# Layer 0's projection as a seven-product Strassen form, with the first phase's other steps moved between engines

## The chip, the cores and the metric

The kernel runs on one core of one Trainium2 chip. A core has five engines with an instruction queue each: TensorE (PE; its weight loads are PEld) multiplies matrices into PSUM, VectorE (DVE) and ScalarE (ACT) work elementwise from SBUF and PSUM, GpSimd (POOL) works elementwise in SBUF, and SyncE (SP) issues most of the DMAs. Each queue runs in its own order; engines wait for one another on semaphores.

The metric is the device time of one execution in microseconds. Before the change it is 2088.59 us, the median of 3 runs (2086.69 to 2091.08).

## What is computed

128 graphs of 128 nodes with 256 features, all float32, pass two layers. Each layer is followed by a residual sum and a layer norm. The change concerns layer 0:

```python
norm = (adj.sum(-1) + 1e-6) ** -0.5                 # per node
f_hom = norm * (adj @ (norm * (x @ theta)))
f_het = x @ W_h
gate  = sigmoid(x @ W_t + b_t)
x1    = layernorm(x + elu(gate * f_hom + (1 - gate) * f_het))
```

Layer 1 takes x1 through a pointwise convolution with batch norm, a convolution of 17 taps along the nodes, a message product weighted by exp(-distance) and a GRU. In this kernel the 17-tap convolution is done in the frequency domain along the nodes.

## The kernel before

**Three phases.** The first (profile time 0 to about 746 us) does layer 0, the pointwise convolution `conv1`, the forward transform (coefficients `H`) and the transform of the convolution weights. The second (to about 960 us) multiplies coefficients and transformed weights, frequency by frequency; its operands come over DMA. The third (to the end) does the inverse transform, messages and the GRU; its GRU projections already use a seven-product Strassen form (`l1_sums`, `l1_gru`, L762 to L805), with 384-column products and with sums on VectorE and GpSimd.

**The first phase's loop** (L436 to L483) runs over turns `t`. A pair `p` is two graphs, so there are 64 pairs, and a turn works on several of them at once, in software pipelining: projection, gate and mix of pair `t`, the rest of layer 0 of pair `t-1`, layer norm, transposition and `conv1` of pair `t-2`, coefficients of pair `t-3`, loads of pair `t+2`, transposition and degrees of pair `t+1`. In about every second turn `w_unit` (L403) transforms one of 32 units of convolution weights: four products on a quarter of the array's rows each (`w_ps`), one for the rest (`wl_ps`), four evictions on ScalarE, one on VectorE. `w_store` writes them out in 16 DMAs a turn later.

**Order.** For TensorE the order is that of the source in all turns (`manual_schedule`). From turn 3 on SyncE, VectorE and ScalarE have the source's order too, while GpSimd is left to the scheduler; in the turns before, a scheduler places all engines but TensorE.

**The projection** (`l0_project`, L291). For each graph, x transposed is multiplied by theta and W_h together (512 columns, `f_ps`) and by W_t (256 columns, `gate_ps`), each over two halves of the 256 features. A float32 product is two passes over the array, so a trace shows two records for each. ScalarE evicts hom, scaled by norm, and het; VectorE adds the gate's bias (L315); ScalarE takes the tanh.

**What follows it.** `l0_mix` (L324) multiplies by adj and scales by norm, less het; `l0_gate` (L339) blends, and takes the minimum and the exponential for elu; `l0_elu` (L348) adds x, then moments and the reciprocal deviation come from `norm_stats` (L242: VectorE statistics, then two small operations on GpSimd in `inv_sqrt`, L150); `norm_apply` (L253) forms the shift `nb` on VectorE and applies it on ScalarE. `l1_turn`, `l1_front` and `l1_analyse` are layer 1's share. `transposed` (L265) turns a pair on TensorE and evicts the result on VectorE (L274), for xT and for x1T.

**Memory.** All PSUM tiles of the phase rotate through 8 banks of one pool:

```python
ps = actx.enter_context(tc.tile_pool(name="psA", bufs=8, space=PSUM, reuse_waits="tile"))
```

x and adjT have four buffers each (`io`), hom, het and gate two; x1 has its own tile with one.

Of the kernel before, what the change touches and what calls it, by code (L numbers as in the profile page):

```python
# [33 lines left out]
def gnn_layers_kernel(ctx: ExitStack, tc: tile.TileContext, a: dict, out: bass.AP):  # L34
# [58 lines left out]
    ps = actx.enter_context(tc.tile_pool(name="psA", bufs=8, space=PSUM, reuse_waits="tile"))  # L93
# [8 lines left out]
    def load(p):  # L102
        s = st[p] = {}
        s["x"] = io.tile([P, J, D], F32, tag="x", name=f"x_{p}")
        nc.sync.dma_start(s["x"], x[p * J : (p + 1) * J].rearrange("b n d -> n b d"))
        s["adjT"] = io.tile([P, J, P], F32, tag="adjT", name=f"adjT_{p}")
        nc.sync.dma_start(s["adjT"], adjT[:, p * J : (p + 1) * J, :])
# [134 lines left out]
    def norm_stats(src, n, name):  # L242

        mv = small.tile([P, n, 2], F32, tag=f"mv{n}", name=f"mv_{name}")
        for q in range(n):
            stats = small.tile([P, 6], F32, tag="stats", name=f"stats_{name}_{q}")
            nc.vector.bn_stats(stats, src[:, q, :])
            nc.vector.bn_aggr(mv[:, q, :], stats)  # L248
        rstd = small.tile([P, n], F32, tag=f"rstd{n}", name=f"rstd_{name}")
        inv_sqrt(rstd, mv[:, :, 1], LN_EPS, n)  # L250
        return mv, rstd

    def norm_apply(src, dst, n, name, mv, rstd):  # L253
        nb = small.tile([P, n], F32, tag=f"nb{n}", name=f"nb_{name}")
        nc.vector.scalar_tensor_tensor(nb, mv[:, :, 0], -1.0, rstd, ALU.mult, ALU.mult)  # L255
        for q in range(n):
            nc.scalar.activation(  # L257
                dst[:, q, :], src[:, q, :], AF.Identity,
                bias=nb[:, q : q + 1], scale=rstd[:, q : q + 1],
            )  # L260
# [4 lines left out]
    def transposed(src, dst, name):  # L265
# [8 lines left out]
        nc.vector.tensor_copy(dst.rearrange("p c n -> p (c n)"), t)  # L274


    def l0_turn(p):
        s = st[p]
        s["xT"] = wk.tile([P, NC, J * P], F32, tag="xT", name=f"xT_{p}")
        transposed(s["x"], s["xT"], f"xT_{p}")  # L280
        deg = bank(f"deg_{p}")
        for j in range(J):
            nc.tensor.matmul(
                deg[:, j : j + 1], lhsT=s["adjT"][:, j, :], rhs=ones[:, 0:1], start=True, stop=True
            )
        norm = s["norm"] = small.tile([P, J], F32, tag="norm", name=f"norm_{p}")
        nc.vector.tensor_copy(norm, deg[:, 0:J])
        inv_sqrt(norm, norm, DEG_EPS, J)


    def l0_project(p, between, beside):  # L291
        s = st[p]
        xT, norm = s["xT"], s["norm"]
        hom = wk.tile([P, J, D], F32, tag="hom", bufs=2, name=f"hom_{p}")
        het = wk.tile([P, J, D], F32, tag="het", bufs=2, name=f"het_{p}")
        gate = wk.tile([P, J, D], F32, tag="gate", bufs=2, name=f"gate_{p}")
        pg = bank(f"gate_ps_{p}")
        for j in range(J):
            if j == 1:
                between()  # L300
            pf = bank(f"f_ps_{p}_{j}")
            for c in range(NC):
                nc.tensor.matmul(  # L303
                    pf, lhsT=xT[:, c, nodes(j)], rhs=w0[:, c, 0 : 2 * D],
                    start=(c == 0), stop=(c == NC - 1),
                )
            for c in range(NC):
                nc.tensor.matmul(  # L308
                    pg[:, j * D : (j + 1) * D], lhsT=xT[:, c, nodes(j)],
                    rhs=w0[:, c, 2 * D : 3 * D], start=(c == 0), stop=(c == NC - 1),  # L310
                )
            nc.scalar.activation(hom[:, j, :], pf[:, 0:D], AF.Copy, scale=norm[:, j : j + 1])  # L312
            nc.scalar.activation(het[:, j, :], pf[:, D : 2 * D], AF.Copy)
        beside()
        nc.vector.tensor_tensor(  # L315
            gate, pg.rearrange("p (j e) -> p j e", j=J),
            b_t.unsqueeze(1).to_broadcast([P, J, D]), ALU.add,
        )

        nc.scalar.activation(gate, gate, AF.Tanh, scale=0.5)  # L320
        s.update(hom=hom, het=het, gate=gate)


    def l0_mix(p):  # L324
        s = st[p]
        adjT_, norm, hom, het = (s[k] for k in ("adjT", "norm", "hom", "het"))
        pm = bank(f"mix_ps_{p}")
        for j in range(J):
            nc.tensor.matmul(  # L329
                pm[:, j * D : (j + 1) * D], lhsT=adjT_[:, j, :], rhs=hom[:, j, :],  # L330
                start=True, stop=True,
            )
        for j in range(J):
            nc.vector.scalar_tensor_tensor(
                hom[:, j, :], pm[:, j * D : (j + 1) * D], norm[:, j : j + 1], het[:, j, :],
                ALU.mult, ALU.subtract,
            )

    def l0_gate(p):  # L339
        s = st[p]  # L340
        hom, het, gate = (s[k] for k in ("hom", "het", "gate"))

        nc.vector.scalar_tensor_tensor(hom, gate, 1.0, hom, ALU.add, ALU.mult)
        nc.vector.scalar_tensor_tensor(het, hom, 0.5, het, ALU.mult, ALU.add)
        nc.vector.tensor_scalar_min(gate, het, 0.0)
        nc.scalar.activation(gate, gate, AF.Exp)

    def l0_elu(p):  # L348
        s = st[p]
        x_, hom, het, gate = (s[k] for k in ("x", "hom", "het", "gate"))  # L350

        nc.vector.scalar_tensor_tensor(gate, gate, -1.0, x_, ALU.add, ALU.add)
        nc.vector.scalar_tensor_tensor(hom, het, 0.0, gate, ALU.max, ALU.add)
        s["stats"] = norm_stats(hom, J, f"a{p}")

    def l0_norm(p):
        s = st[p]
        s["x1"] = wk.tile([P, J, D], F32, tag="x1", name=f"x1_{p}")
        norm_apply(s["hom"], s["x1"], J, f"a{p}", *s["stats"])


    def l1_turn(p):
        s = st[p]
        s["x1T"] = wk.tile([P, NC, J * P], F32, tag="x1T", name=f"x1T_{p}")
        transposed(s["x1"], s["x1T"], f"x1T_{p}")

    def l1_front(p):
        s = st[p]
        h = s["h"] = wk.tile([P, J, D], F32, tag="h", name=f"h_{p}")
        for j in range(J):  # L370
            ph = bank(f"conv1_ps_{p}_{j}")
            for c in range(NC):
                nc.tensor.matmul(  # L373
                    ph[:, 0 : D + CO], lhsT=s["x1T"][:, c, nodes(j)], rhs=conv1_w[:, c, :],
                    start=(c == 0), stop=(c == NC - 1),
                )
            nc.vector.tensor_tensor(h[:, j, :], ph[:, 0:D], shift1, ALU.add)
            nc.scalar.activation(coords[:, p * J + j, :], ph[:, D : D + CO], AF.Copy)
        nc.scalar.activation(h, h, AF.Relu)

    def l1_store(p):
        s = st[p]
        nc.sync.dma_start(x1_d[p], s["x1"].rearrange("p j e -> p (j e)"))
# [19 lines left out]
    def w_unit(u):  # L403
        t = wt[u % NW].rearrange("p i o -> p (i o)")
        pq = [bank(f"w_ps_{u}_{r}") for r in range(4)]
# [24 lines left out]


# [4 lines left out]
    for t in range(-1, NP + 3):  # L436
        with tc.manual_schedule(engines={E.PE, E.SP, E.DVE, E.Activation} if t > 2 else {E.PE}):
# [5 lines left out]
            def between():  # L443
                on(t - 1, l0_gate)
                on(t - 3, l1_analyse)

            def beside():
                on(t - 1, l0_elu)

            on(t - 2, l1_turn)  # L450
            if 0 <= t < NP:
                l0_project(t, between, beside)
            else:
                between()
                beside()
            on(t - 1, l0_norm)
# [10 lines left out]
            on(t - 2, l1_front)  # L467
# [5 lines left out]
            on(t + 1, l0_turn)  # L473
# [301 lines left out]
    def l1_gru(g, pr):  # L775
# [47 lines left out]
        norm_apply(y, y, 2, f"b{g}_{pr}", *norm_stats(y, 2, f"b{g}_{pr}"))  # L823
# [78 lines left out]
```

## Time and profile before

| | |
|---|---|
| median of 3 runs | 2088.59 us |
| the profiled execution, whole | 2086.79 us |
| its span, first to last instruction | 2085.0 us |
| granted TensorE clock, mean | 0.994 |
| TensorE busy, 20 to 720 us / 720 to 746 us | 694.38 / 17.85 us |
| TensorE busy, 746 to 960 us / 960 to 2070 us | 207.54 / 1110.00 us |
| VectorE / ScalarE / GpSimd busy, 20 to 720 us | 518.55 / 399.65 / 110.88 us |

Busy times come from hardware records of one profiled execution; engines overlap, so they don't add up to the span. A matmul's end is modelled, and matmuls run in a pipeline: what one costs is read from the start of one to the start of the next. An entry "[0.70 <-ACT gate L346]" in a row says that the engine stood idle for 0.70 us before it, and that ScalarE's instruction of line 346 ended the wait. Lines are those of the kernel before; rows of helpers (`inv_sqrt`, `norm_stats`, `transposed`) carry the helper's line.

### The profile page before, as it was taken

To read this page: it belongs to the slowest core of one execution; us is meant where nothing else is said; L and a number is where in the kernel's file an instruction comes from. 1 tells how busy PE (TensorE), PEld (TensorE's weight loads), DVE (VectorE), ACT (ScalarE), POOL (GpSimd) and SP (SyncE) were. 2 spreads that over 40 slices of the span, in tenths; PEclk is the share of its full clock that TensorE was granted. 3 is DMA by queue.
4 is the path that set the end of the run, shared out by engine and by line. 5 is a ranking of instruction groups with operands and counts; after the bars stand their busy time and mean duration, and the time that the engine had idled before them with its cause. 6 is when DMAs were issued, how large, how long until landed. Compare 5 with 4: busy or idle time off the path is not lost.

```text
span 2085.0 us, 27437 instructions
## 1 busy us (share of the span) xinstructions
PE 2043.7 (98%) x9025; PEld 1401.6 (67%) x9025; DVE 1433.0 (69%) x2856; ACT 744.0 (36%) x1484; POOL 672.9 (32%) x889
## 2 busy tenths in 40 slices
PE   8999999999999979999999999999999999999997
PEld 5666666766667658886666666666666666666664
DVE  7777777776777744447776766676767767766766
ACT  3555555555555511112222222222222222222221
POOL 1111111111111135553343444343434434443432
PEclk9999999999999999999999999999999999999999
DMA  3444444344444469993222122212212221221100
GB/s 117 137 145 138 137 147 144 133 144 137 140 145 133 153 228 318 305 302 119 62 82 68 54 74 72 69 60 72 78 51 75 70 73 56 67 72 56 36 25 21
DMA packets 191789, 235.39 MB, mean 113 GB/s; under 512 B 16400, under 2 KB 136736, under 8 KB 191648
## 3 DMA queue, kind: packets, MB, share of 16 engines
q1 hardware_dynamic: 186160, 229.44, 33.5%
q10 hardware_dynamic: 5488, 4.21, 0.7%
q8 instruction: 72, 1.18, 0.2%
q14 instruction: 69, 0.57, 0.1%
HBM read 129.77 MB, written 103.81 MB: 112 GB/s over the span
## 4 chain that ended last, share of the span: by engine, by line
PE 95%; DVE 2%; DMA 2%; ACT 1%; issue 1%; POOL 0%; POOLq 0%; ACTq 0%; DVEq 0%; SPq 0%
PE g_ps L784 42%; PE f_ps L303 10%; PE msg_ps L703 5%; PE gate_ps L308 5%; PE conv_ps L373 5%; PE y_ps L510 5%; PE mix_ps L329 3%; PE coef_ps L391 3%; PE nmp_ps L754 3%; PE conv_ps L669 3%; PE z_ps L523 2%; PE w_ps L408 2%; PE x1T_ps L270 2%; PE wl_ps L411 1%; PE xT_ps L270 1%; PE dist_ps L739 1%
## 5 line engine op out<-in xcount | busy, mean ns | idle before, releaser
L303 PE MATMUL f_ps<-w,xT 128*128 128x512 f32 x512 | 244.1, 600 | 0.1
L808 ACT ACTIVATE o<-o 128x1024 f32<-128x1024 f32 x64 | 67.6, 1057 | 335.6 <-DVE o L805 335.6
L152 POOL TENSOR_SCALAR rstd_b<-mv_b 128x2 f32<-128x2 f32 x64 | 12.2, 191 | 501.6 <-DVE mv_b L248 501.6
L152 POOL TENSOR_SCALAR rstd_a<-mv_a 128x2 f32<-128x2 f32 x64 | 12.2, 191 | 463.9 <-DVE mv_a L248 447.9
L784 PE MATMUL g_ps<-t_c,sc 128*128 128x384 f32 x384 | 155.2, 486 | 0.0
L784 PE MATMUL g_ps<-t_m,sm 128*128 128x384 f32 x384 | 155.2, 486 | 0.0
L784 PE MATMUL g_ps<-t_h,sh 128*128 128x384 f32 x384 | 155.2, 486 | 0.0
L257 ACT ACTIVATE y<-y,nb_b,rstd_b 128x256 f32<-128x256 f32 x128 | 69.9, 593 | 218.6 <-DVE nb_b L255 218.6
L308 PEld LDWEIGHTS gate_ps<-w,xT 128*128 128x128 f32 x512 | 98.2, 192 | 69.2 <-issue 61.8
L510 PE MATMUL y_ps<-wb,H 128*128 128x256 f32 x544 | 128.9, 380 | 4.7 <-DMA wb<-w_d 2.1
L308 PE MATMUL gate_ps<-w,xT 128*128 128x256 f32 x512 | 132.2, 381 | 0.0
L802 POOL TENSOR_TENSOR u<-u,p 128x512 f32<-128x512 f32 x64 | 81.1, 1267 | 155.4 <-DVE p L801 155.4
L303 PEld LDWEIGHTS f_ps<-w,xT 128*128 128x128 f32 x512 | 88.6, 192 | 62.6 <-issue 62.2
L312 ACT ACTIVATE hom<-f_ps,norm 128x256 f32<-128x256 f32 x128 | 60.5, 473 | 187.0 <-PE f_ps L303 187.0
L518 POOL TENSOR_TENSOR ws<-wb 128x512 f32<-128x512 f32 x67 | 94.8, 1416 | 88.7 <-PE z_ps L523 60.3
L373 PE MATMUL conv_ps<-conv_w,x1T 128*128 128x259 f32 x512 | 122.6, 381 | 0.0
L510 PEld LDWEIGHTS y_ps<-wb,H 128*128 128x128 f32 x544 | 102.8, 190 | 20.5 <-issue 5.1
L703 PE MATMUL msg_ps<-w_msgT_w,cx1T 128*128 128x256 f32 x512 | 115.6, 379 | 0.0
L784 PEld LDWEIGHTS g_ps<-t_m,sm 128*128 128x128 f32 x384 | 73.0, 190 | 50.9
L784 PEld LDWEIGHTS g_ps<-t_c,sc 128*128 128x128 f32 x384 | 73.0, 190 | 50.9
L784 PEld LDWEIGHTS g_ps<-t_h,sh 128*128 128x128 f32 x384 | 72.9, 190 | 50.9 <-issue 1.2
L373 PEld LDWEIGHTS conv_ps<-conv_w,x1T 128*128 128x128 f32 x512 | 97.2, 190 | 14.4
(219 smaller groups left out, 4622.4 us busy)
## 6 DMA issues: line engine op xcount, KB each, us to landing
wb<-w_d SPq DMA_DIRECT2D x68, 512.0 KB
w_d<-w_o SPq DMA_DIRECT2D x256, 128.0 KB
y_d<-yb SPq DMA_DIRECT2D x68, 256.0 KB
x<-in_x SPq DMA_DIRECT2D x64, 256.0 KB
x_d<-x SPq DMA_DIRECT2D x64, 256.0 KB
x1T_d<-x1T SPq DMA_DIRECT2D x64, 256.0 KB
cx1T<-x1T_d SPq DMA_DIRECT2D x64, 256.0 KB
yt<-y_d SPq DMA_DIRECT2D x32, 512.0 KB
```

The costliest lines, as they stand in the source:

```text
L257: nc.scalar.activation(dst[:, q, :], src[:, q, :], AF.Identity, bias=nb[:, q : q + 1], scale=rstd[:, q : q + 1],)
L270: nc.tensor.transpose(t[:, (c * J + j) * P : (c * J + j + 1) * P], src[:, j, c * P : (c + 1) * P], ident,)
L303: nc.tensor.matmul(pf, lhsT=xT[:, c, nodes(j)], rhs=w0[:, c, 0 : 2 * D], start=(c == 0), stop=(c == NC - 1),)
L308: nc.tensor.matmul(pg[:, j * D : (j + 1) * D], lhsT=xT[:, c, nodes(j)], rhs=w0[:, c, 2 * D : 3 * D], start=(c == 0), stop=(c == NC - 1),)
L329: nc.tensor.matmul(pm[:, j * D : (j + 1) * D], lhsT=adjT_[:, j, :], rhs=hom[:, j, :], start=True, stop=True,)
L373: nc.tensor.matmul(ph[:, 0 : D + CO], lhsT=s["x1T"][:, c, nodes(j)], rhs=conv1_w[:, c, :], start=(c == 0), stop=(c == NC - 1),)
L510: nc.tensor.matmul(py[:, blk, :], lhsT=coefs(blk if k == 0 else 2 * k + 1 - blk, c), rhs=w[:, c, blk, :], start=(c == 0), stop=(c == NC - 1),)
L518: nc.gpsimd.tensor_tensor(ws, w[:, :, 0, :], w[:, :, 1, :], ALU.add)
L703: nc.tensor.matmul(pm[:, j * D : (j + 1) * D], lhsT=x1T[:, c, nodes(q)], rhs=w_msg[:, c, :], start=(c == 0), stop=(c == NC - 1),)
L784: nc.tensor.matmul(pg[:, lo : lo + 3 * P], lhsT=s[f"f{kind}"][i][:, pr, :], rhs=factors[kind][i], start=(k == 0), stop=(k == 2), skip_grou ...
L802: nc.gpsimd.tensor_tensor(u4, u2, p5, add)
L808: nc.scalar.activation(rz, rz, AF.Tanh, scale=0.5)
```

## The change

Seen as 2 x 2 blocks of 128, the two graphs' transposed features (two graphs x two feature halves) times the weights (two feature halves x two halves of the output features, with theta, W_h and W_t beside each other: 3 x 128 = 384 columns) is one 2 x 2 block product. It is now computed by seven products of 128 x 384. The right factors are formed once (`right_factors`, on VectorE), the left factors for each pair (`left_factors`, on GpSimd). Two of the seven sums are made by accumulation in PSUM (products 1 onto "a" and 2 onto "c"), five on VectorE. ScalarE copies "a" twice.

Further: adj is scaled by norm in SBUF on GpSimd (`l0_scale`) in place of scaling hom in its eviction; the gate's bias goes to GpSimd, in two halves; so do the minimum and nb; the evictions of xT and x1T go from VectorE to ScalarE; x1 is normalised in place in x's tile, so that the load of pair p+4 into it follows the store of pair p; adjT has three buffers; PSUM is split into four rotating banks and one bank each for a, b, c, d, which `w_unit` uses too; GpSimd joins the engines with a fixed order from turn 3 on; and the order within a turn is written anew. `norm_stats` and `norm_apply` are shared with the third phase, which gets its nb from GpSimd as well.

```diff
-        nc.vector.tensor_copy(dst.rearrange("p c n -> p (c n)"), t)
+        nc.scalar.activation(dst.rearrange("p c n -> p (c n)"), t, AF.Copy)
...
+    def left_factors(t, a11, a12, a21, a22, engine):
+        engine.tensor_tensor(t[:, 0], a21, a22, ALU.add)
+        engine.tensor_tensor(t[:, 1], t[:, 0], a11, ALU.subtract)
+        engine.tensor_tensor(t[:, 2], a11, a21, ALU.subtract)
+        engine.tensor_tensor(t[:, 3], a12, t[:, 1], ALU.subtract)
+        return a11, a12, t[:, 3], a22, t[:, 0], t[:, 1], t[:, 2]
...
+    def l0_scale(p):
+        inv_sqrt(norm, norm, DEG_EPS, J)
+        nc.gpsimd.tensor_tensor(
+            s["adjT"], s["adjT"], norm.unsqueeze(2).to_broadcast([P, J, P]), ALU.mult
         )
...
+    def l0_product(p, i, of, add=False):
...
+        nc.tensor.matmul(
+            ps_[of][:, 0 : 3 * P], lhsT=st[p]["left"][i], rhs=f0[i],
+            start=not add, stop=True, skip_group_check=True,
+        )
+    def l0_sum(p):
...
+        nc.scalar.activation(u1, f_ps(p, "a"), AF.Copy)
+        nc.vector.tensor_tensor(u2, f_ps(p, "b"), u1, ALU.add)
+    def l0_sums(p):
...
+        nc.vector.tensor_tensor(u3, f_ps(p, "b"), u2, ALU.add)
+        nc.vector.tensor_tensor(o[:, 1, 1, :], f_ps(p, "c"), u3, ALU.add)
+        nc.vector.tensor_tensor(o[:, 1, 0, :], u3, f_ps(p, "d"), ALU.subtract)
+        nc.scalar.activation(o[:, 0, 0, :], f_ps(p, "a"), AF.Copy)
+    def l0_last(p):
...
+        nc.vector.tensor_tensor(s["o"][:, 0, 1, :], f_ps(p, "c"), s["u2"], ALU.add)
...
+    def l0_bias(p, j):
+        g = st[p]["gate"][:, 2 * j : 2 * j + 2, :]
+        nc.gpsimd.tensor_tensor(g, g, b_t.rearrange("p (h e) -> p h e", h=2), ALU.add)
...
+        nc.gpsimd.tensor_scalar(s["gate"], s["het"], 0.0, None, ALU.min)
...
+        nc.vector.scalar_tensor_tensor(r, s["gate"], -1.0, r, ALU.add, ALU.add)
+        nc.vector.scalar_tensor_tensor(r, s["het"], 0.0, r, ALU.max, ALU.add)
```

The new order within a turn:

```diff
+            product(0, "a")
+            product(5, "b")
+            product(4, "c")
+            on(t - 1, l0_gate)
+            on(t, l0_sum)
+            on(t - 2, l0_norm)
+            on(t - 1, l0_het)
+            on(t - 3, l1_analyse)
+            on(t - 1, l0_exp)
             on(t - 2, l1_turn)
+            product(6, "b")
+            product(1, "a", True)
+            product(3, "d")
+            on(t, l0_sums)
+            on(t - 1, l0_elu)
+            on(t, lambda p: l0_bias(p, 1))
...
+            on(t + 1, l0_turn)
+            on(t - 1, l0_stats)
+            on(t - 2, lambda p: l1_front(p, 0))
+            product(2, "c", True)
+            on(t, l0_last)
+            on(t, lambda p: l0_bias(p, 0))
+            on(t - 2, lambda p: l1_front(p, 1))
+            on(t, l0_tanh)
+            on(t - 1, l0_rstd)
+            on(t + 1, l0_scale)
+            on(t - 2, l1_relu)
             on(t - 2, l1_store)
```

The line numbers that the prediction gives for new instructions (L360 for o01, L373 for the bias, L412 and L413 for elu) are those of the changed kernel.

## The prediction

> **What bounds the kernel now.** I read the page first, then the busy time by stretch, then one turn of the first phase on TensorE, VectorE and GpSimd.
>
> ```profile
> PE 2043.7 (98%) x9025; PEld 1401.6 (67%) x9025; DVE 1433.0 (69%) x2856; ACT 744.0 (36%) x1484; POOL 672.9 (32%) x889
> ```
> ```profile
> 20.00:720.00 700.00, 694.38 (x3285) 474.10 (x3284) 518.55 (x1153) 399.65 (x927) 110.88 (x250) 1.00 0.41 138
> 960.00:2070.00 1110.00, 1110.00 (x4649) 730.16 (x4648) 777.34 (x1407) 293.26 (x441) 436.50 (x519) 1.00 0.19 62
> ```
>
> Columns of the second view: stretch, length, then busy time of PE, PEld, DVE, ACT, POOL. TensorE fills 99% of the first phase (20 to 720 us) at full clock; VectorE is the next, 74%; GpSimd has 16%. So time is to be had by giving TensorE less, as long as no other queue then comes to set the pace. A turn without a unit of `w_unit` ("plain") and one with it ("w turn") mostly alternate: the formula of `units` gives 28 pairs and 3 w turns that follow a w turn. A plain turn on TensorE:
>
> ```profile
> 403.88 1.88 PE L303 MATMUL f_ps<-w,xT 128*128 128x512 f32 x4
> 405.60 1.03 PE L308 MATMUL gate_ps<-w,xT 128*128 128x256 f32 x4
> 406.46 1.09 PE L391 MATMUL coef_ps<-A,h 128*128 128x136 f32 x8
> 407.39 1.88 PE L303 MATMUL f_ps<-w,xT 128*128 128x512 f32 x4
> 409.11 1.03 PE L308 MATMUL gate_ps<-w,xT 128*128 128x256 f32 x4
> 409.97 1.91 PE L373 MATMUL conv_ps<-conv_w,x1T 128*128 128x259 f32 x8
> 411.72 0.60 PE L270 MATMUL xT_ps<-ident,x 128*128 128x128 f32 x4
> 412.16 0.50 PE L283 MATMUL deg<-ones,adjT 128*128 128x1 f32 x4
> 412.52 1.11 PE L329 MATMUL mix_ps<-hom,adjT 128*128 128x256 f32 x4
> ```
>
> The durations overlap, so a stage's cost is start to start: projection 2 x (1.72 + 0.86) = 5.16 us. From the first f_ps of this turn to that of the next (413.91) is 10.03 us, and over the following w turn (426.13) 12.22: **22.25 us for a pair**.
>
> **What the change takes from TensorE.** 7 products of 384 columns instead of 8 x 512 + 8 x 256 column passes. The last phase has the same product shape, started every 0.645 us (2050.16, 2050.81, 2051.45): 7 x 0.645 = 4.51 instead of 5.16, **0.645 us a turn**. For the 61 turns from the third on that is 39 us, and a pair that TensorE alone sets would take 20.96 us.
>
> **What it puts elsewhere, per turn.** VectorE loses two 512-column evictions (0.69, 0.68), the bias (0.69), the minimum (0.43), nb (0.16) = 2.65 us, and gets five sums of 384 columns; the row of that size is 551 ns: 2.75. Equal. ScalarE loses four evictions (1.70) and gets two of 512 columns (0.60 each, L414) and two of 384 (about 0.5): +0.5, on an engine that is 57% busy. GpSimd gets four factors of 128 columns (a 256-column sum takes 0.73, one of 512 1.27, so about 0.46), two biases of 256 (0.73), adj's scaling (0.73), the minimum (between 0.65 and 1.27, no row; I take 0.65, as it has one input) and two tiny ones: 1.77 becomes about 7.3 us. SyncE gets no instruction, but since x is normalised in place, the load of x (L105) now waits for the landing of the store of the x four turns back, just issued; behind it stand adjT's load and 16 w stores (10.2 us of issue in a pair). SyncE is busy some 14 of 22 us, and the store of x1T ahead of the load waits longer anyway: nothing, at most 2 us of its slack.
>
> **Where the path goes.** In the built program VectorE's queue in a turn is: sum u2, het, u3, o11, o10, two of elu, norm, statistics, h, o01 (L360), h, mix, gate. The sum o01 feeds the second mix product; yet it stands behind elu and statistics, which stand behind o10, which waits for the product "d". The trace has that stretch:
>
> ```profile
> 407.26 0.69 DVE L352 SCALAR_TENSOR_TENSOR gate<-gate,x 128x512 f32<-128x512 f32 x1 [0.70 <-ACT gate L346]
> 407.98 0.69 DVE L353 SCALAR_TENSOR_TENSOR hom<-het,gate 128x512 f32<-128x512 f32 x1
> 408.71 0.43 DVE L247 BATCH_NORM_STATS2 stats_a<-hom 128x6 f32<-128x256 f32 x1
> 409.17 0.18 DVE L248 BATCH_NORM_AGGREGATE mv_a<-stats_a 128x2 f32<-128x6 f32 x1
> 409.27 0.39 DVE L247 BATCH_NORM_STATS2 stats_a<-hom 128x6 f32<-128x256 f32 x1
> 409.70 0.18 DVE L248 BATCH_NORM_AGGREGATE mv_a<-stats_a 128x2 f32<-128x6 f32 x1
> ```
>
> 2.62 us to 409.88. With o10 0.47 before it, norm 0.08, h 0.35 and o01 0.55 after it: **4.07 us from "d" to o01**. TensorE meanwhile has xT 0.44, degrees 0.36, two conv1 1.75, product "c" 0.645, first mix 0.47 = 3.66. So it waits. In plain turns the built order sets the next turn's "a" and "b" ahead of the second mix product, which covers 1.3 us; not in w turns. I follow the chain from o01 to o01:
>
> - Plain to w turn: bias L373 on GpSimd 0.73 (rstd stands behind it in the queue), rstd and nb 1.45 (410.04 to 411.01 for rstd, two tiny ones more), normalisation on ScalarE 1.08, x1T 0.44, products b, a, d 1.93, hand-over to VectorE 0.20 (conv1 ends 411.72, h starts 411.92), 4.07, other hand-overs 0.15: 10.05.
> - w to plain turn: second mix 0.47, w_unit 2.19 (12.22 - 10.03), a, b, c 1.93, coef 0.93, x1T 0.44, b, a, d 1.93, 0.20, 4.07, 0.05: 12.21.
>
> Together **22.26 us, against 22.25 before**: what TensorE saves turns into a wait for o01 and one for the normalisation.
>
> **The rule that speaks against it.** The row first, of the last phase, where both engines have two-input work:
>
> ```profile
> 1188.43 0.69 DVE L815 SCALAR_TENSOR_TENSOR o<-o 128x512 f32<-128x512 f32 x1 [1.18 <-ACT o L808]
> 1189.04 0.95 DVE L770 TENSOR_TENSOR sm<-nmpT 128x256 f32<-128x256 f32 x1
> 1189.91 1.52 DVE L816 SCALAR_TENSOR_TENSOR o<-o 128x512 f32<-128x512 f32 x1
> ```
> ```profile
> 1188.57 1.13 POOL L771 TENSOR_TENSOR sh<-cx1T,sh 128x256 f32<-128x256 f32 x1
> 1189.72 2.61 POOL L729 TENSOR_TENSOR own<-turned,mask 128x512 f32<-128x512 f32 x2
> ```
>
> L770 takes 0.95 beside GpSimd's sum (0.42 alone), L816 1.52 (0.69 alone); L815, which got there first, pays nothing and GpSimd's sum grows from 0.73 to 1.13. It looks like one after the other. The Trainium skill (GPSIMD Engine Reference, section 1, Specifications) says that GpSimd shares its SBUF interfaces with VectorE, and that instructions of VectorE with two SBUF inputs contend. The rule gives no price: by its engine-selection table (4.1, elementwise work belongs on VectorE, GpSimd about twice as slow) I would count only GpSimd's longer times, 22.26 a pair; the rows add a price on VectorE. Both elu operations (L412, L413) have two SBUF inputs and start just as GpSimd begins the bias and four factors, 2.5 us of work. By the rows the first goes free, the second waits for one GpSimd operation: about 0.53 if that is 256 columns wide, about 0.25 if it is a factor. Ends 0 and 0.53; I take 0.3, near the narrower operation, because the factors are four of those five. It lies wholly on both chains: +0.6 a pair. 28 x 0.61 + 3 x 0.3 = **+18 us**.
>
> **The start.** The eviction of xT was VectorE's at 5.26 us; it is now ScalarE's first compute, behind its DMA issues:
>
> ```profile
> 8.80 0.78 ACTq L138 DMA_DIRECT2D vec<-in_L_gnn_bn_b  x2
> 9.87 1.28 ACT L312 ACT_TABLE_LOAD   x1 [9.87 <-PE f_ps L303]
> ```
>
> 9.58 + 1.28 + 0.6 = 11.5 us instead of 5.95 for the first product: 5.5 late. The narrower products return about 1 of it at the slow clock of the start (one pass of 512 columns takes 0.85 us there, 0.43 later); the batch-norm chain (L207, then 3.4 us of TensorE wait) stands behind them and is not overlapped. The four right factors on VectorE (4 x 0.55) lie under ScalarE's delay. I take +4, between 2 and 6.
>
> **The rest.** Drain of the first phase: minimum and nb on GpSimd in an exposed chain, +0.5. The last phase loses nb from VectorE, which waits 61 us there for GpSimd, but TensorE is busy 1110 of 1110 us, so that is worth nothing; at the very end nb costs 0.2 more.
>
> **Sum.** 18 + 4 + 0.5 = +22 us: span 2107, profiled run about 2109 (1.8 us lie around the span), and about **2110 us** for the median, which is 1.8 over the profiled run.
>
> **Rivals.**
> - *The chain holds, but the engines don't contend in this place* (VectorE goes first each time, GpSimd pays): 22.26 a pair, only start and drain are left: 2093. For it: L815 paid nothing. Against it: L770 paid in nearly all of its 32 (median 0.946). 0.20.
> - *TensorE stays the bound*: the scheduler's order, or shorter hand-overs, hide o01. -39 + 4: 2053. It decides if "d" to o01 takes under 3.66 + 1.29 us in plain turns and, in w turns, no more than 3.66; the 2.62 us of elu and statistics alone leave 1.04 for o10, h and o01, which need 1.45. So it fails by 0.4 us without any contention, unless the four-bank rotation and hand-overs are kinder than I count. 0.10, with half-way cases.
> - *GpSimd sets the pace*: 7.3 us of a turn of about 11, plus the 2.8 us of two-input operations that VectorE holds the way for, is near full; then minimum, exp and left factors come late too. Both elu operations pay 0.53 and GpSimd's own run 15% longer: 1.4 a pair, 2130 or more. 0.15.
> - *The order isn't what the source says*: the built order already departs from it in plain turns only, to the good. This is in my sum.
>
> The forecast has 0.55. The range 2083 to 2130 runs from the no-contention case with hand-overs 0.2 us shorter per turn (-11 + 3) to GpSimd's case, and leaves out TensorE's. The likeliest case alone is 2098 to 2122. A measurement can tell about 0.2%, 4 us, from no change: faster 0.15 (TensorE's, and part of the no-contention case), same 0.12, slower 0.73.
>
> **What would show it.** Right: TensorE's share in 40 to 700 us falls to about 93%, the second mix product of w turns waits for VectorE (o01) about 1 us and x1T for ScalarE; the second elu operation is longer than the first 0.69; GpSimd about 65% busy there; first product at about 11.5 us. Wrong: pairs of 21 us with TensorE at 99%, or elu at 0.69 both times, or GpSimd never idle in a turn.

## The result and the profile after

| | before | after |
|---|---|---|
| median of 4 runs each | 2088.74 us | 2167.94 us (2166.66 to 2169.71) |
| the profiled execution, whole / its span | 2086.79 / 2085.0 us | 2169.03 / 2167.2 us |
| span up to the first product of turn 3 | 42.5 | 57.1 |
| turn 3 to turn 63 | 676.7 | 738.8 |
| turn 63 to the first product of the second phase | 26.9 | 32.6 |
| from there to the end | 1338.9 | 1338.7 |

The ratio is 1.0379 (95% interval 1.0361 to 1.0397): 79 us slower, where the forecast had 22. The spans differ by 82.2 us: 14.7 before turn 3, 62.1 in the turns, 5.7 in the drain, nothing behind it. The forecast's terms for these were 4, 18, 0.5 and 0.2. (Times in this document count from the first instruction. The expectations below count turn 3's start from the profiler's own zero, some 11 us earlier: their 53.4 and 68.1 us are the 42.5 and 57.1 of the table.)

The page of the kernel after, its totals and the engines' shares of the chain of waits:

```profile
PE 2050.3 (95%) x8897; PEld 1380.7 (64%) x8897; DVE 1439.9 (66%) x2796; ACT 771.6 (36%) x1484; POOL 1111.8 (51%) x1657
...
PE 73%; POOL 12%; DVE 6%; DMA 3%; issue 2%; ACT 2%; SPq 2%; POOLq 0%; ACTq 0%; DVEq 0%
```

And the stretch of the first phase, columns as in the prediction (stretch, length, PE, PEld, DVE, ACT, POOL):

```profile
20.00:720.00 700.00, 629.39 (x2833) 406.75 (x2834) 487.52 (x1058) 382.76 (x829) 465.86 (x782) 0.99 0.37 123
```

TensorE fell from 99 to 90% of the stretch, GpSimd rose from 16 to 67%, and no engine is full. That points to waits in a ring rather than to one overloaded engine. The steady turns, read from the first product of one turn to that of the next, are mostly 9.06 us (plain) and 14.8 (w turn): **23.88 us a pair** on the mean of turns 25 to 40, against 22.25 before and 22.86 in the forecast (22.26 and twice 0.3).

Which ring? Take the o01 chain of the prediction on this trace. From plain to w turn, GpSimd with ScalarE's row between (line numbers of the kernel after; start, length):

```profile
511.43 0.55 DVE L360 TENSOR_TENSOR o<-f_ps_c,u 128x384 f32<-128x384 f32 x1
...
512.05 0.73 POOL L373 TENSOR_TENSOR o<-o,L_gnn_b_t_b 128x256 f32<-128x256 f32 x1
...
512.87 0.19 POOL L152 TENSOR_SCALAR rstd_a<-mv_a 128x2 f32<-128x2 f32 x1
...
513.14 0.73 POOL L153 TENSOR_TENSOR rstd_a<-rstd_a,neg_half 128x2 f32<-128x2 f32 x1
...
513.95 0.24 POOL L256 TENSOR_SCALAR nb_a<-mv_a 128x2 f32<-128x2 f32 x1
...
514.27 0.68 POOL L257 TENSOR_TENSOR nb_a<-nb_a,rstd_a 128x2 f32<-128x2 f32 x1
...
514.99 1.09 ACT L262 ACTIVATE x<-x,nb_a,rstd_a 128x256 f32<-128x256 f32 x2 [1.02 <-POOL nb_a L257]
```

The bias starts 0.07 us after o01's end, and from its start to the normalisation's it is 2.94 us; the forecast had 0.73 + 1.45 = 2.18. From o01 to the next o01 (522.72) it is 11.29, and from w to plain turn 12.59: together 23.88, the whole pair. So the forecast's chain is closed in this trace. But a second queue is just as full. SyncE in another pair of the kernel after; a gap between rows is a wait:

```profile
406.70 0.37 SPq L448 DMA_DIRECT2D x_d<-x  x1
407.17 0.38 SPq L449 DMA_DIRECT2D x1T_d<-x1T  x1
408.77 0.38 SPq L105 DMA_DIRECT2D x<-in_x  x1
409.25 0.42 SPq L107 DMA_DIRECT2D adjT<-in_adjT  x1
409.72 1.48 SPq L116 DMA_DIRECT2D wt<-in_conv_wT  x4
411.30 0.91 SPq L448 DMA_DIRECT2D x_d<-x  x1
412.83 0.35 SPq L449 DMA_DIRECT2D x1T_d<-x1T  x1
418.73 0.38 SPq L105 DMA_DIRECT2D x<-in_x  x1
```

and the same two stores and the load behind them in the kernel before:

```profile
416.58 0.38 SPq L383 DMA_DIRECT2D x_d<-x  x1
417.06 0.38 SPq L384 DMA_DIRECT2D x1T_d<-x1T  x1
417.49 0.46 SPq L105 DMA_DIRECT2D x<-in_x  x1
```

Before, the load follows at once. After, it waits 1.22 us in one turn and 5.55 in the other, until the x stored just ahead of it has landed in HBM, because x is now normalised in place and the load writes over it. All 16 w stores (10.4 us of issue) follow only then. Over turns 25 to 40 SyncE has, per pair, 14.9 us of issue, 1.5 of short gaps between issues and 7.0 of waits for these landings: 23.4 of the 23.88, so it is all but full. In 60 to 760 us (who waits, for what: sum, times, longest):

```profile
SPq L105 <- DMA x_d<-x: 197.3, 55, 6.3
```

This trace alone cannot say which of the two rings sets the turn. Nor can it say whether a single wait on TensorE (x1T for the normalisation, conv1 for x1T, mix for o01, product a for w_o) matters.

### The profile page after: what moved, and what is told of

The parts are those of the page before. It is cut to its first block, busy times and chain, and to the rows that moved or that the text cites. A ratio compares the mean times of both kernels' runs of the same rounds, so it can differ in the third digit from the quotient of the medians.

```text
span 2167.2 us, 28134 instructions
## 1 busy us (share of the span) xinstructions
PE 2050.3 (95%) x8897; PEld 1380.7 (64%) x8897; DVE 1439.9 (66%) x2796; ACT 771.6 (36%) x1484; POOL 1111.8 (51%) x1657
## 3 DMA queue, kind: packets, MB, share of 16 engines
q8 instruction: 72, 1.18, 0.2%
## 4 chain that ended last, share of the span: by engine, by line
PE 73%; POOL 12%; DVE 6%; DMA 3%; issue 2%; ACT 2%; SPq 2%; POOLq 0%; ACTq 0%; DVEq 0%
PE g_ps L869 40%; PE y_ps L595 5%; PE msg_ps L788 5%; PE nmp_ps L839 3%; PE conv_ps L754 2%; PE z_ps L608 2%; POOL o L399 2%; PE f_ps_a L334 2%; PE f_ps_c L334 2%; PE f_ps_b L334 2%; PE conv_ps L435 2%; DVE x L412 2%; POOL norm L153 2%; POOL o L373 1%; PE dist_ps L824 1%
## 5 line engine op out<-in xcount | busy, mean ns | idle before, releaser
L152 POOL TENSOR_SCALAR rstd_b<-mv_b 128x2 f32<-128x2 f32 x64 | 12.2, 191 | 503.7 <-DVE mv_b L248 503.7
L435 PE MATMUL conv_ps<-conv_w,x1T 128*128 128x259 f32 x512 | 140.6, 398 | 17.9 <-ACT x1T L279 17.4
L373 POOL TENSOR_TENSOR o<-o,L_gnn_b_t_b 128x256 f32<-128x256 f32 x128 | 105.9, 828 | 79.9 <-DVE o L355 70.3
L887 POOL TENSOR_TENSOR u<-u,p 128x512 f32<-128x512 f32 x64 | 81.0, 1265 | 106.3 <-DVE p L886 106.3
L399 POOL TENSOR_SCALAR o<-o 128x512 f32<-128x512 f32 x64 | 96.0, 1499 | 66.1 <-DVE o L398 61.9
L334 PE MATMUL f_ps_a<-w,xT 128*128 128x384 f32 x256 | 109.0, 508 | 15.0 <-ACT w_o L479 9.6
L334 PE MATMUL f_ps_b<-t,sx 128*128 128x384 f32 x256 | 107.4, 502 | 4.6 <-POOL sx L291 2.6
L869 PE MATMUL g_ps<-w_hhT_w,cx1T 128*128 128x384 f32 x256 | 105.1, 492 | 0.0
L869 PE MATMUL g_ps<-w_ihT_w,nmpT 128*128 128x384 f32 x256 | 103.6, 486 | 0.2 <-ACT nmpT L843 0.2
```

What stands on the lines that cost most here:

```text
L334: nc.tensor.matmul(ps_[of][:, 0 : 3 * P], lhsT=st[p]["left"][i], rhs=f0[i], start=not add, stop=True, skip_group_check=True,)
L373: nc.gpsimd.tensor_tensor(g, g, b_t.rearrange("p (h e) -> p h e", h=2), ALU.add)
L399: nc.gpsimd.tensor_scalar(s["gate"], s["het"], 0.0, None, ALU.min)
L435: nc.tensor.matmul(ph[:, 0 : D + CO], lhsT=s["x1T"][:, c, nodes(j)], rhs=conv1_w[:, c, :], start=(c == 0), stop=(c == NC - 1),)
L869: nc.tensor.matmul(pg[:, lo : lo + 3 * P], lhsT=s[f"f{kind}"][i][:, pr, :], rhs=factors[kind][i], start=(k == 0), stop=(k == 2), skip_grou ...
L887: nc.gpsimd.tensor_tensor(u4, u2, p5, add)
```

## Experiments

"Pair" below is a plain turn and the w turn after it, mean of turns 25 to 40, in us. Times are medians with the ratio to the kernel before on the same chip (2085 to 2087 us) and its interval. All but the control of the kernel before are of two runs, so gains under some 5 us are read from the traces only.

### One wait of the chain at a time

**The minimum, back to VectorE:**

```diff
-        nc.gpsimd.tensor_scalar(s["gate"], s["het"], 0.0, None, ALU.min)
+        nc.vector.tensor_scalar_min(s["gate"], s["het"], 0.0)
```

> The minimum of elu goes back from GpSimd to VectorE. Theory 1 (GpSimd's late results hold up ScalarE's queue, and by it conv1): the minimum takes 0.43 us instead of 1.50, exp starts 1 us or more earlier, the time falls by 0.5 us a turn, to 2120-2150 us, and conv1's wait for x1T (17.4 us) goes. Theory 2 (the sum o01, behind elu and statistics on VectorE, and contention set the pace, as the forecast had it): VectorE gets 0.43 us more in the chain, so 2165-2195 us.

2169.2 us (1.0395, 1.0331 to 1.0458), pair 23.91. Theory 1 as stated fails: conv1's wait for x1T falls to 1.7 us in 100 to 760 us as it said, yet nothing is gained, since waits for u (8.1) and x's load (5.6) come in its place. The time lies in theory 2's range.

**The fourth factor in a tile of its own:**

```diff
-        t = wk.tile([P, 4, P], F32, tag="sx", name=f"sx_{p}")
+        t = wk.tile([P, 3, P], F32, tag="sx", name=f"sx_{p}")
+        t3 = wk.tile([P, P], F32, tag="sx3", name=f"sx3_{p}")
...
-        engine.tensor_tensor(t[:, 3], a12, t[:, 1], ALU.subtract)
+        engine.tensor_tensor(last, a12, t[:, 1], ALU.subtract)
```

> The fourth left factor, the only one that product c still reads late, gets a tile of its own; the other three no longer wait for product c. Theory 1 (normalisation and adj's scaling come late on GpSimd because 1.85 us of factors start only after product c): three factors move up, the wait of sx for f_ps_c (81.5 us) falls under 30 us, the normalisation comes 1.4 us earlier, time 2125-2155 us. Theory 2 (elu and o01 set the pace): the factors now start beside elu and lengthen both its operations; 2165-2185 us.

2162.7 us (1.0363, 1.0333 to 1.0393), pair 23.78. GpSimd's wait for product c, 72.3 us in 60 to 760 us before, falls to about 1, but o01, which the bias needs, depends on product c as well: the normalisation moves no earlier. The time is under theory 2's range and far over theory 1's: the wait was in plain view and cost next to nothing.

**Both:**

> Both edits together. Theory 1: what the forecast left out is gone, so the time comes to the forecast plus the longer start: 2105-2130 us, TensorE 94 to 96% busy in 100 to 700 us. Theory 2: at least 2150 us. If only one of the two waits binds at a time, the sum is smaller than the two single gains together.

2163.0 us (1.0365, 1.0335 to 1.0395), pair 23.54. Theory 1 fails again, and theory 2 holds.

**o01 ahead of the statistics on VectorE:**

```diff
-            on(t - 1, l0_stats)
             on(t - 2, lambda p: l1_front(p, 0))
             product(2, "c", True)
             on(t, l0_last)
+            on(t - 1, l0_stats)
```

> The changed kernel with one move: the statistics' four operations (1.1 us) stand behind the sum o01 on VectorE instead of ahead of it. Theory 1 (o01's place in VectorE's queue makes TensorE wait): the wait of mix for o01 (9.8 us in 100-760 us) goes, and with the bias 1.1 us earlier a pair falls by 1.2-1.5 us: 2120-2135 us. Theory 2 (GpSimd is then next: bias stands behind the four factors, which wait for product c): only mix's 0.65 us in turns with a unit is gained, 2145-2155 us. Theory 3 (neither binds): within 5 us of 2167.

2172.4 us (1.0412, 1.0381 to 1.0443), pair 23.79. Mix's wait for o01 goes (12.2 to 2.3 us in 60 to 820 us) and w turns fall from 14.8 to 13.9, but product a's wait for the w_o eviction rises from 8.2 to 27.9, and plain turns grow to between 9.5 and 11.3. By the time it is nearest to theory 3, by the waits to theory 2.

**GpSimd: rstd and nb ahead of the bias that waits for o01** (on the run with the minimum on VectorE and the fourth factor apart):

```diff
-            on(t, lambda p: l0_bias(p, 0))
-            on(t - 2, lambda p: l1_front(p, 1))
-            on(t, l0_tanh)
             on(t - 1, l0_rstd)
+            on(t, lambda p: l0_bias(p, 0))
+            on(t - 2, lambda p: l1_front(p, 1))
+            on(t, l0_tanh)
```

> Like the run with minimum and fourth factor changed, and on GpSimd rstd and nb stand ahead of the bias that waits for o01. Theory 1 (the chain o01, bias, rstd, nb, normalisation, x1T through GpSimd, 2.94 us from bias to normalisation where the forecast had 2.18): the normalisation no longer waits for o01, x1T's wait for it goes, a pair falls from 23.5 to 22.3-22.8 us, time 2120-2140 us. Theory 2 (o01 late for the second mix product is the whole of it): no gain, and tanh comes 1.3 us later, 2160-2180 us.

2176.4 us (1.0431, 1.0401 to 1.0462), pair 24.68: theory 2's side. The wait of x1T is gone, but tanh is late, relu and w_o stand behind it on ScalarE, and TensorE waits for h (46.5 us in 60 to 820 us) and w_o (29.0).

**The biases on VectorE, and left out:**

```diff
-        nc.gpsimd.tensor_tensor(g, g, b_t.rearrange("p (h e) -> p h e", h=2), ALU.add)
+        nc.vector.tensor_tensor(g, g, b_t.rearrange("p (h e) -> p h e", h=2), ALU.add)
```

> The changed kernel with both biases on VectorE (0.4 us each there, 0.83 on GpSimd). Theory 1 (GpSimd's line): rstd starts 0.7 us earlier, elu runs at 0.69 us, against 0.4 us more ahead of o01: 2145-2160 us. Theory 2 (o01's place on VectorE): o01 comes later by one bias less what elu gains, so 2165-2180 us.

2190.4 us (1.0504, 1.0469 to 1.0539), pair 24.83, worse than either theory. Waits of TensorE in 100 to 760 us (sum, times, longest):

```profile
PE coef_ps L456 <- ACT h L444: 57.4, 25, 2.4
```

tanh now waits for a VectorE that is busy with elu and statistics, and relu's result is late for the coefficients.

In the next run the kernel leaves the gate's bias out, so its result is another one and only its time counts:

> The changed kernel without the two additions of the gate's bias on GpSimd (this part of the result is left out). Theory 1 (GpSimd's line sets the normalisation and tanh): rstd starts 0.8 us earlier, tanh no longer waits for GpSimd, and the two elu operations, beside which GpSimd now has nothing until product c is done, take 0.69 us each instead of 0.92 and 0.90: 1.2-2.0 us a pair, 2110-2135 us. Theory 2 (the wait for o01 and contention only): 0.4 us a turn from elu, 2140-2150 us. If neither: within 5 us of 2167.

2157.7 us (1.0347, 1.0317 to 1.0377), pair 23.84: in none of the three ranges. The two elu operations without a GpSimd operation beside them, and below them the first of the two in the kernel after (groups of 60 to 760 us: count, busy, mean ns, idle before):

```profile
L413 DVE SCALAR_TENSOR_TENSOR x<-o,x 128x512 f32<-128x512 f32 x57 | 39.4, 692 | 1.9
L412 DVE SCALAR_TENSOR_TENSOR x<-o,x 128x512 f32<-128x512 f32 x57 | 39.4, 691 | 4.0
```
```profile
L412 DVE SCALAR_TENSOR_TENSOR x<-o,x 128x512 f32<-128x512 f32 x57 | 52.4, 919 | 5.0 <-ACT o L407 4.4
```

So contention costs 0.23 us on the mean in each (the second has 907 ns), 0.44 a turn; the forecast had 0.3. W turns (13.3) gain here and plain turns (10.1 to 11.1) lose as much: theory 1's gain appears in one turn and is gone in the next.

### Three together

> Three of the edits at once: minimum on VectorE, the fourth factor in a tile of its own, o01 ahead of the statistics. Theory 1 (several chains through the fixed orders are within 1 us of each other, so each edit alone only uncovers the next: after o01 it was product a's wait for w_o, behind tanh, bias and factors, and conv1's for x1T, behind exp and the minimum; together they go): a pair falls from 23.9 to 21.8-22.6 us, time 2105-2130 us. Theory 2 (a chain that none of them touches sets the pace, through contention on VectorE or PSUM banks): 2150 us or more.

2171.0 us (1.0411, 1.0381 to 1.0441): theory 1 fails by 40 us, although w turns are now 12.1 to 13.9 us (14.8). Plain turns take 9.8 to 14, without a pattern, and the pair is 24.24. The waits in 60 to 760 us (who waits, for what: sum, times, longest) name DMAs:

```profile
DVE wl_o L483 <- DMA w_d<-wl_o: 67.2, 18, 5.2
...
PE xT_ps L275 <- DMA x<-in_x: 9.3, 19, 1.5
```

wl_o waits for SyncE's stores of the unit before, and x comes late. SyncE waits 201.1 us for the landings (197.3 in the kernel after). The pair is 23.5 us or more whatever is done to the chain: that points to a second wall, which all these runs have in common.

### SyncE's queue

**Five buffers for x.** The load then writes over an x whose store was issued a turn earlier. Room comes from the w tiles, two instead of three:

```diff
-        s["x"] = io.tile([P, J, D], F32, tag="x", name=f"x_{p}")
+        s["x"] = io.tile([P, J, D], F32, tag="x", bufs=5, name=f"x_{p}")
...
-    NW = 3
+    NW = 2
...
                 w_store(units[t - 1])
+                if units[t - 1] + 2 < NU:
+                    w_load(units[t - 1] + 2)
...
-                if units[t] + 2 < NU:
-                    w_load(units[t] + 2)
                 w_unit(units[t])
```

> The changed kernel with five buffers for x instead of four (their room comes from w_load's tiles, two instead of three, loaded a turn later), so that SyncE's load of x no longer waits for the landing of the store just issued. In the trace of after SyncE has hardly a gap in a pair: 10.4 us of w stores, 4.9 of other issues, waits of 1.2 and 5.5 for the landing, of 23.9. Theory 1 (two walls at nearly the same height: SyncE's queue at about 23.5 us a pair, the chain of VectorE, GpSimd and ScalarE at 23.9): alone it changes only the places where SyncE is behind, so wl_o's wait for w_d (29.4 us) falls under 10 us, and the time is 2145-2162 us with pairs still at 23.9. Theory 2 (SyncE's wait is all of it): pairs of 22.3 us or less, under 2125 us. Theory 3 (SyncE costs nothing, as the forecast had it): within 4 us of 2167.

2159.6 us (1.0358, 1.0328 to 1.0388), pair 24.02: theory 1. SyncE's waits for x's store are gone from the list, wl_o's for w_d falls to 2.6 us, and turns 3 to 63 take 725.2 instead of 738.8. Most of that is at the three places where a unit follows a unit (turns 3 to 5, 22 to 24, 41 to 43): 116.5 us instead of 127.8; before has 110.5. Most regular turns are as long as in the kernel after (9.05 and 14.84), and SyncE is now the one that waits for ScalarE's results (its own waits in 60 to 760 us):

```profile
SPq L448 <- ACT x L262: 121.2, 28, 8.5
SPq L449 <- ACT x1T L279: 74.4, 28, 3.0
```

So in the regular turns of the kernel after the chain sets the pace, with SyncE close below it; where a unit follows a unit, SyncE is behind. Of the 13.6 us gained in the turns, 4.4 are lost again behind them, in the second phase, for a reason that was not looked for.

**The three edits of the chain and five x:**

> Minimum on VectorE, fourth factor in a tile of its own and o01 ahead of the statistics (together within 5 us of 2167 without this), and five buffers for x. Theory 1 (two walls): now both are lower, pairs of 21.4-22.3 us, 2085-2115 us. Theory 3 (SyncE costs nothing; a chain that no edit has touched keeps pairs at 23.5): 2160-2172 us.

2122.6 us (1.0180, 1.0151 to 1.0210), pair 22.57, turns 3 to 63 in 686.0. The time is 8 us over theory 1's upper end, and theory 3 is out by 38 us: five x buffers give 8 us alone, the three edits none, both together 45. That is what two walls of nearly the same height do. Which of the three edits lowers the chain, once SyncE's waits are gone, was not tried one by one.

**The wait alone, in the kernel before:**

```diff
-        s["x1"] = wk.tile([P, J, D], F32, tag="x1", name=f"x1_{p}")
-        norm_apply(s["hom"], s["x1"], J, f"a{p}", *s["stats"])
+        norm_apply(s["hom"], s["x"], J, f"a{p}", *s["stats"])
...
-        transposed(s["x1"], s["x1T"], f"x1T_{p}")
+        transposed(s["x"], s["x1T"], f"x1T_{p}")
```

and the store takes x.

> The kernel before with the one thing that makes SyncE wait: the normalised block is written into x instead of a tile of its own, so that the load of x four turns on waits for the store's landing. By the issues in the trace of before (15.3 us a pair) plus waits of 6.7 us, SyncE would need 22.0 of the 22.25 us of a pair. Theory 1: it is just under the bound there, and only places where one unit follows another lose: 2089-2105 us, with waits of wl_o for w_d. If the wait alone were the wall of after (theory 2): pairs of 23 us or more, over 2110 us. Theory 3: 2084-2090 us.

2143.8 us (1.0282, 1.0252 to 1.0312), pair 23.47: **58 us**, what theory 2 said of this kernel and not what theory 1 did, though five buffers for x alone ruled theory 2 out for the changed kernel, where the chain is a wall too. The longest wait of a compute engine for a DMA in 60 to 760 us, and SyncE's own first:

```profile
DVE wl_o L416 <- DMA w_d<-wl_o: 68.2, 21, 12.7
```
```profile
SPq L105 <- DMA x_d<-x: 211.2, 57, 6.4
```

No engine got more to do here, nothing in GpSimd's or VectorE's order changed. My 22.0 us for SyncE were too low. On the mean of turns 25 to 40 this trace has 14.7 us of issue, 1.4 of short gaps and 7.2 of waits: 23.3 of the 23.47. In one pair the waits are 1.7 and 5.8, and from one w store group to the next it is 24.0.

**The control, the same with five x:**

> The control of the kernel before with its normalisation in place (2143.8 us): the same with five buffers for x, so that the load's wait falls on a store issued a turn earlier. If the 58 us are SyncE's wait for the landing: 2084-2095 us, pairs at 22.25. If the normalisation in place costs by something else (the transposes read another tile, ScalarE writes what VectorE read): over 2120 us.

2085.05 against 2084.91 us, ratio 1.0002 (0.9992 to 1.0012; 10 and 11 runs), pair 22.25. The 51 regular turns take 566.2 us in both. So the normalisation in place costs nothing by itself that these runs could tell, and the 58 us are the load's wait for a store just issued.

### The other terms

**The minimum alone, in the kernel before** (the same replacement, the other way round).

> The kernel before with nothing but its minimum moved to GpSimd (there the 512 columns lie in one piece, in the changed kernel in four pieces of 128). If the operation itself is slow there: about 1.5 us. If the four pieces make it slow: about 0.65 us. The time, where TensorE has 98%: 2085-2100 us either way.

2103.7 us (1.0080, 1.0051 to 1.0110), 3.7 over the expected. GpSimd's row in 100 to 700 us, tile in one piece:

```profile
L345 POOL TENSOR_SCALAR gate<-het 128x512 f32<-128x512 f32 x52 | 77.6, 1492 | 153.4 <-DVE het L344 153.4
```

In the changed kernel, with four pieces, it is 1.50: the layout is not it. The 17 us are an operation 1.06 us longer on an engine that is mostly idle: 11.7 lie in turns 3 to 63, where the w turn takes 12.57 us instead of 12.22 and the plain turn the same 10.03, 2.8 ahead of turn 3 and 2.5 in the drain. In the w turn it is `w_unit`'s four products that take longer, 1.42 us instead of 1.07 from their start to that of the next product. Why was not tested.

**Units never one after the other:**

```diff
-    units = {2 + u * (NP - 5) // (NU - 1): u for u in range(NU)}
+    units = {2 + 2 * u: u for u in range(NU)}
```

> The changed kernel with a w_unit in every second turn (2, 4, ... 64), so that none follows another directly. In the trace the three places where one follows another cost 5 to 9 us more than in the kernel before, with a wait of f_ps_a for w_o of up to 5.4 us there. If that is the cause (the eviction of w_o waits for w_d's stores, and product a for its bank): 12-20 us less, 2148-2156 us, and the wait of f_ps_a for w_o in 100-760 us (8.2) goes. If it is another: within 5 us of 2167; a unit now ends the phase, +2 us.

2161.7 us (1.0361, 1.0331 to 1.0391), between the two forecasts. The irregular turns vanish, every pair is 23.9, and the waits of wl_o and w_o on w_d with them; so the 17.3 us lost at those three places come from a unit that follows a unit. Five buffers for x took away 11.3 of them, so that much is SyncE falling behind. But a unit lies in the drain here, and the second phase's first product waits 9.7 us for w_d: the drain is 8.8 us longer.

**The start.** First GpSimd in the written order from the first turn on, then the first three blocks' xT evictions, factors and biases on VectorE:

```diff
-        with tc.manual_schedule(engines={E.PE, E.SP, E.DVE, E.Activation, E.Pool} if t > 2 else {E.PE}):
+        with tc.manual_schedule(engines={E.PE, E.SP, E.DVE, E.Activation, E.Pool} if t > 2 else {E.PE, E.Pool}):
```

> The changed kernel with GpSimd in the written order from the first turn on instead of from turn 3. In the trace of after the first two biases and rstd of turns 1 and 2 stand behind adj's scaling and the factors, and TensorE waits 3.0 us for the normalisation of turn 2, and its clock falls after it. If GpSimd's order costs the start: turn 3 begins at 58-63 us instead of 68, time 2157-2162. If the first evictions cost it: turn 3 begins at 66-69 us and the time stays within 3 us.

```diff
-        transposed(s["x"], xT, f"xT_{p}")
+        transposed(s["x"], xT, f"xT_{p}", p < 3)
...
-            t, *(xT[:, c, nodes(j)] for j in range(J) for c in range(NC)), nc.gpsimd
+            t, *(xT[:, c, nodes(j)] for j in range(J) for c in range(NC)), nc.vector if p < 3 else nc.gpsimd
```

> The changed kernel, where only blocks 0 to 2 have xT's eviction, the four factors and the biases on VectorE. In after turn 3 starts at 68.1 us, in before at 53.4. Theory 1 (the start's 14.7 us, forecast as 4, are xT's eviction behind ScalarE's issues, 5.5 us, and GpSimd's line ahead of the first normalisation, about 9): turn 3 starts at 54-60 us, time 2153-2160 us. Theory 2 (the loss is in what stays: minimum, order, unit in turn 2): turn 3 at 63 us or later, 2162 us or more.

(the biases likewise). 2167.8 us (1.0390, 1.0360 to 1.0420), turn 3 at 58.0 (69.0 as the expectations count); and 2162.0 us (1.0365, 1.0321 to 1.0409), turn 3 at 53.5 (64.7): the second theory in both. Order is not it, and evictions, factors and biases together are 3.7 of the 14.7 us. Turn 2, the first w turn, takes 18.8 to 22.9 us in these, 20.2 in the kernel after, 11.3 before, and 15.3 where the biases are left out. The start is not settled.

**Loads first, and everything together:** `on(t + 2, load)` stands at the head of the turn.

> The run with three edits and five buffers for x (2122.6 us), and the loads of x and adjT stand first in SyncE's turn, ahead of the stores that wait for ScalarE. There TensorE waits 13.2 us for x in 60-760 us and ScalarE 24.7 us for the store of x1T. If what is left in the pairs (22.2 us on the mean) is SyncE's order: the wait for x goes, 2105-2115 us. If it is VectorE's queue: 2120-2125 us.

> All edits: minimum on VectorE, fourth factor apart, o01 ahead of the statistics, five x with the loads first, and the first three blocks on VectorE. If the gains add: 2095-2108 us, still above before; under 2080 only if pairs come to 21.3 us.

2137.0 us (1.0245, 1.0216 to 1.0275) and 2135.8 us (1.0240, 1.0205 to 1.0274): both miss. At the head of the turn the load again meets a store that is still in flight (SyncE waits 154.5 us for x_d in 60 to 760 us), and x1T's store stands behind it (ScalarE waits 69.6 us for it). No version here beats the kernel before; 2122.6 us is the best of the changed kind.

## Why the prediction was wrong

- **The direction and the gain of TensorE** were right: products start every 0.645 us (516.51, 517.16, 517.80 in the kernel after), and TensorE fell to 90% (forecast 93).
- **The first step that failed: "SyncE is busy some 14 of 22 us, and the store of x1T ahead of the load waits longer anyway: nothing, at most 2 us of its slack."** The 14 us of issue were right; the term put at nothing is the wait for the landing. It took the length of that wait from the store's place, not from its landing. Measured, the two landings in a pair take SyncE 7.0 us (1.22 and 5.55 in the pair shown) on top of 14.9 us of issue and 1.5 of short gaps, which is 23.4 of a pair of 23.88. Alone this costs 58 us in the kernel before, with the control at 1.0002. In the changed kernel removing it gives 8 us alone and 48 once the chain is shortened (2171.0 to 2122.6).
- **The second: the o01 chain, 22.86 us a pair, was right in kind and short by 1.02.** This alone would have failed the forecast too: with five buffers for x, SyncE's wait is gone, the pair still stands at the chain's 24.02, and the time is 2159.6 us, 50 over the forecast. From w to plain turn the chain is 12.59 against 12.51 with contention. From plain to w turn it is 11.29 against 10.35: 0.76 of the 0.94 lie between bias and normalisation on GpSimd, 2.94 where I had 2.18. The term is "rstd and nb 1.45": nb's two operations, "two tiny ones", took 0.24 and 0.68, with some 0.08 us of hand-over before each step. The 0.68 (L257, 514.27) ran beside VectorE's gate (L394, 514.21 to 514.90); in every second turn, without it, L257 takes 0.20. So GpSimd, too, pays beside VectorE; the forecast's sum had a price on VectorE alone. Another 0.25, net, lies between o10 and o01: an exp that is 0.18 late by the minimum, and 1.18 us for an elu operation where I took 0.69 + 0.3.
- **How much each is of the loss.** The spans differ by 82.2 us, 59.5 more than the forecast's terms. The 51 regular turns lost 44.8 us where the forecast's 18 were for all turns: the chain is about 27 of the 59.5. The three irregular places lost 17.3, of which five buffers for x take away 11.3. The start is 10.7 and the drain 5.2.
- **"GpSimd minimum 0.65"** was wrong: 1.50 us, over even my upper end of 1.27. Put back on VectorE alone it changed nothing in the turns, since SyncE's wall stood. GpSimd's sum was also added up wrong: its terms, with 0.24 for a tiny operation as in the chain, come to 6.9 us and not 7.3. Measured are 7.9 a turn (67% of 11.94), 0.85 of it the longer minimum.
- **Contention on VectorE** was about right: 0.44 us a turn against 0.3, and one of the two elu operations pays, as the last phase's rows said.
- **The start**: the first product came at 11.50 us (forecast 11.5), but 14.7 us were lost by turn 3 against 4. Some 5.5 of it are the late first product. Turn 2 takes 20.2 us instead of 11.3; TensorE waits 3 us there for the normalisation and runs slower after it. What makes the turn so long, the experiments left open.
- **The drain** cost 5.7 instead of 0.5. That was not tested.
- **The rival "GpSimd sets the pace"** named the right symptoms (minimum, exp and factors late), and the result lies in its open range (2130 or more), but not for its reason: GpSimd is idle a third of the phase, and minimum and factors, relieved while SyncE's wall stood, gave no more than 5 us. Once SyncE's waits are gone, relieving them and moving o01 gives 37 us (2159.6 to 2122.6). How much of that is GpSimd's and how much is o01's place was not measured. "TensorE stays the bound" was nowhere near: pairs of 20.96 were never reached, the best of the changed kind is 22.57.

Of the 36.1 us (spans) that the kernel with both walls lowered still loses, 12.9 are before turn 3, 9.3 in the turns, 7.9 in the drain, and 6.0 behind it. None of these is explained.

## What to carry to other kernels

Cost each queue as a ring of its own, the DMA queue too: issue times plus the waits in front of them must fit in a turn, and a buffer that is read by a store and then loaded again on the same queue puts the store's landing, not its issue, into that ring. When removing one visible wait after another gives nothing, look for what the runs have in common, and lower two walls in one run: 8 and 0 us alone were 45 together here. A run that gains nothing does not show that the wait it removes is harmless, as long as another ring of the same length stands. Reusing a tile in place looks free by every engine's busy time, so ask which queued instruction has to wait for its last reader.

## What the hardware showed besides

- A minimum of one operand over 128x512 takes GpSimd 1.50 us in the kernel after, in four pieces, longer than the two-input sums of that size in the same profile (L887, mean 1265 ns). In one piece (the minimum alone in the kernel before) it takes 1.49.
- The same 256 KB store lands early or late by what was issued ahead of it: from the issue's start to the load that waits for it, 2.07 us behind the w stores (406.70 to 408.77), and 7.43 us behind the loads of x, adjT and the w tile, 520 KB (411.30 to 418.73). The amount does not explain the 7.43: from 414.70 to 417.20 us the DMA engines moved 22 GB/s at a share of 0.07, about one of 16, so most of them had nothing left to do. What the one was busy with, and whether another place for the w tile's four loads would shorten the wait, was not tested.
- After a wait of 3.0 us in turn 2 TensorE ran at half its speed for a while (kernel after; the same products start 0.645 us apart elsewhere):

```profile
44.48 0.33 PE L275 MATMUL x1T_ps<-ident,x 128*128 128x128 f32 x1 [3.00 <-ACT x L262]
...
45.66 1.49 PE L334 MATMUL f_ps_b<-t,sx 128*128 128x384 f32 x2
46.95 1.43 PE L334 MATMUL f_ps_a<-w,xT 128*128 128x384 f32 x2
```

Product a starts 1.29 us after product b, and the granted clock in 44 to 49 us is 0.66. So this wait cost more than its own length.
